# A four-layer graph network on one core: source logits taken from the projection, sums placed one chunk later, and a normalisation moved to ScalarE

## The chip, the core and the metric

The kernel runs on one core of a Trainium2 chip. The metric is the device time of one execution in microseconds (us); less is better. The engines of the core have short names in the profile: PE is TensorE (matmul), PEld its weight loads, DVE is VectorE, ACT is ScalarE, POOL is GpSimd, SP is SyncE, which here only issues transfers. A "q" behind a name (SPq, ACTq) means the sequencer that feeds the engine.

## What is computed

A graph with N = 2708 nodes and 256 features goes through four layers; each adds its result to the features and normalises the rows. Only layers 1 and 3 are touched by the change (layer 0 matters because layer 1's projection is computed inside its loop). Cut to that:

```python
x = layernorm(x + adj @ (x * W0))                        # layer 0
# layer 1: attention with 4 heads of 64 columns
h   = (x @ W).reshape(n, heads, head_dim)
src = einsum('nhd,d->nh', h, a[:head_dim, 0])            # source logits
dst = einsum('nhd,d->nh', h, a[head_dim:, 0])            # target logits
e   = src[:, :, None] + dst.T[None, :, :]
e   = where(e > 0, e, 0.2 * e)                           # leaky relu
attn = softmax(where(adj[:, None, :] > 0, e, -9e15))
out  = einsum('nhm,mhd->nhd', attn, h)
x = layernorm(x + layernorm(out) * gamma + beta)
# ... layer 2: a signed graph attention with 3 heads and two GRU cells ...
# layer 3
h = adj @ (x @ neigh_W.T) / (adj.sum(1) + 1)
x = layernorm(x + concatenate([x, h]) @ lin_W.T)
```

The 2708 nodes are 22 tiles of 128 rows (P = 128; the last tile has 20). adj is 2708 x 2708 and is read several times from the chip's main memory.

## The kernel before

It is a kernel in which each stage has been tuned by hand; a scheduler behind the language may move an instruction within the order of its engine, so the order in a trace is not always that of the text.

**Layer 1's softmax without a maximum.** Since exp(leaky(s + d)) is the larger of exp(s + d) and exp(0.2 (s + d)), a weight can be written, up to a factor of the row, as max(exp(-0.8 s), exp(0.8 d)) times exp(0.2 d). The kernel calls exp(-0.8 s) `fall` (one number per row and head, needed as a *row* that is spread over all partitions, `fall_b`), exp(0.8 d) `rise` (one number per partition) and folds exp(0.2 d) into the projected features `hs`. `fall` is therefore stored to a small array `fall_d` (4 x 2708) in main memory and loaded again, spread over 128 partitions.

**The projection of a tile, inside layer 0's loop** (`w1_a` holds, side by side, 4 columns for the source logits, 256 for the features and 4 for the target logits; H = 4, F = 256, FC = 2 blocks of 128):

```python
def layer1_projection(pool, t):
    n = sz(t)
    xt = transposed(ps_t, pool, xs[t], n, "xt")          # 2 PE transposes (tr), 1 ACT copy (L165)
    pm = ps_m.tile([P, 2 * F], F32, tag="pm", name="pm")
    for f in range(FC):
        nc.tensor.matmul(
            pm[:n, : F + H], xt[:, f, :n], w1_a[:, f, H:], start=(f == 0), stop=(f == FC - 1)
        )
    nc.scalar.activation(rise[:n, t, :], pm[:n, F : F + H], AF.Exp, scale=1.0 - ALPHA)
    nc.scalar.activation(hs[t][:n, :, HD], pm[:n, F : F + H], AF.Exp, scale=ALPHA)
    nc.vector.tensor_tensor(hs[t][:n, :, :HD], ...)
    pf = ps_t.tile([P, 4, P], F32, tag="tr", name="pf")
    for f in range(FC):
        nc.tensor.matmul(
            pf[:, 0, :n], w1_a[:, f, :P], xt[:, f, :n], start=(f == 0), stop=(f == FC - 1)
        )
    fall = pool.tile([H, P], F32, tag="fall", name="fall")
    nc.scalar.activation(fall[:, :n], pf[:H, 0, :n], AF.Exp, scale=ALPHA - 1.0)
    nc.gpsimd.dma_start(fall_d[:, t * P : t * P + n], fall[:, :n])
    # ... at the end of a span of tiles: load_fall(...) spreads fall_d over the partitions ...
```

In layer 0's loop TensorE does for each tile the strip (22 matmuls of 128x256, line 199), then the previous tile's tr, pm and pf. `load_strip` brings a strip of adj (1408 KB) into one of two buffers.

**Layer 1's main loop.** For two spans of target rows at a time (up to 1024 columns; three such groups), for two pairs of heads (`q`), over 22 chunks `c`:

```python
for c in range(NT):
    for i in range(2):                                    # DVE, L668
        nc.vector.scalar_tensor_tensor(p[:, :w], falls[g // 2][:, 2 * q + i, :w],
            rise[:, c, 2 * q + i : 2 * q + i + 1], mask[:, c, at : at + w], ALU.max, ALU.mult)
    for part in (heads, totals)[:: 1 if c % 2 == 0 else -1]:
        part(c, ps, ...)                                  # PE, L650 (acc) and L659 (den)
    step(c)                                               # one piece of the row work, below
    if c % 5 == 4 and degrees:
        row_degree(degrees.pop(0))                        # two ACT passes over a row of adj
```

**The row work between the chunks.** While a group runs, the rows that the group before has finished are normalised, and a part of layer 2 is prepared from them: for each tile its features times two vectors give u (128 x 3), u is split into three bfloat16 parts, and the edge mask P (a row of 2708, copied from fp8 to bfloat16) is multiplied with them ("the sums over P u", line 490, six matmuls named `pu`). Two buffers hold mask rows in turn. `step(c)` advances a generator; each `yield` is one chunk:

```python
def layer1_logits(pool, t, m, fill, split, gap):
    xt = transposed(ps_t, pool, xs[t], n, "xt")
    nc.gpsimd.dma_start(xt_d[g][:, :, at : at + n], xt[:, :, :n])
    fill(m, t)                                            # ACT, L560: the mask row of the tile
    yield
    own = m[:n, t * P : t * P + n]
    nc.vector.tensor_tensor(own, own, offdiag_h[:n, :n], ALU.mult)        # L573
    # ... pm (L576) = xt times uw on PE, u (L580) copied by ACT
    for i in range(3):                                    # L584, L587: five small operations
        split.tensor_copy(part, left)
        if i < 2:
            split.tensor_tensor(r[:n], left, part, ALU.subtract)
    for _ in range(gap):
        yield
    edge_part(t, m)                                       # PE, L490

if q == 1 and c % 2 == 0 and c // 2 < len(halves):        # in step(c): one tile every two chunks
    t = ended[c // 2][0]
    rows = two_rows[t % 2]
    steps.append(itertools.chain(
        halves[c // 2], [None], layer1_logits(l1, t, rows, mask_row, nc.gpsimd, 2)))
```

**Layer 3's rows.** When a block of layer 3 is summed up, its columns are turned back into rows and normalised (`moments` gives mean and 1 / standard deviation; the power -0.5 is on GpSimd, L151):

```python
pt = bank()
for f in range(FC):
    nc.tensor.transpose(pt[:n, f * P : (f + 1) * P], src[:, f, :n], ident)
nc.vector.scalar_tensor_tensor(o[:n], pt[:n, :F], rdeg[:n, t : t + 1], o[:n], ALU.mult, ALU.add)
layernorm(o, o, n)    # moments, then L157 on DVE: (o - mean) * rs
(nc.gpsimd if t % 2 else nc.sync).dma_start(out[t * P : t * P + n, :], o[:n])
```

Of the kernel before, what the change touches and what calls it, by code (L numbers as in the profile page):

```python
# [9 lines left out]
F32 = mybir.dt.float32  # L10
# [4 lines left out]
AF = mybir.ActivationFunctionType  # L15
ALU = mybir.AluOpType
# [3 lines left out]
P = 128  # L20
NEG_INF = -9000000000000000.0
HIGHEST = 3.0e38
ALPHA = 0.2
# [4 lines left out]
def kernel(  # L28
# [114 lines left out]
    def moments(src, n):  # L143

        bst = small.tile([P, 6], F32, tag="bn_st", name="bn_st")
        nc.vector.bn_stats(bst[:n], src[:n])
        mv = small.tile([P, 2], F32, tag="bn_mv", name="bn_mv", bufs=12)
        nc.vector.bn_aggr(mv[:n], bst[:n])
        rstd = small.tile([P, 1], F32, tag="bn_rs", name="bn_rs", bufs=12)
        nc.vector.tensor_scalar(rstd[:n], mv[:n, 1:2], EPS, None, ALU.add)  # L150
        nc.gpsimd.tensor_tensor(rstd[:n], rstd[:n], neg_half[:n], ALU.pow)  # L151
        return mv[:n, 0:1], rstd[:n]

    def layernorm(dst, src, n):

        mean, rs = moments(src, n)
        nc.vector.tensor_scalar(dst[:n], src[:n], mean, rs, ALU.subtract, ALU.mult)  # L157
# [154 lines left out]
    if True:  # L312
# [14 lines left out]
        if True:  # L327
# [5 lines left out]
# [3 lines that stand above are left out]
                pm = ps_m.tile([P, 2 * F], F32, tag="pm", name="pm")  # L336
                for f in range(FC):
                    nc.tensor.matmul(  # L338
                        pm[:n, : F + H], xt[:, f, :n], w1_a[:, f, H:], start=(f == 0), stop=(f == FC - 1)
                    )  # L340
                nc.scalar.activation(rise[:n, t, :], pm[:n, F : F + H], AF.Exp, scale=1.0 - ALPHA)
                nc.scalar.activation(hs[t][:n, :, HD], pm[:n, F : F + H], AF.Exp, scale=ALPHA)
                nc.vector.tensor_tensor(
                    hs[t][:n, :, :HD],
                    pm[:n, :F].rearrange("p (h d) -> p h d", d=HD),
                    hs[t][:n, :, HD:].to_broadcast([n, H, HD]),
                    ALU.mult,
                )
                pf = ps_t.tile([P, 4, P], F32, tag="tr", name="pf")
                for f in range(FC):  # L350
                    nc.tensor.matmul(
                        pf[:, 0, :n], w1_a[:, f, :P], xt[:, f, :n], start=(f == 0), stop=(f == FC - 1)
                    )
                fall = pool.tile([H, P], F32, tag="fall", name="fall")
                nc.scalar.activation(fall[:, :n], pf[:H, 0, :n], AF.Exp, scale=ALPHA - 1.0)
                nc.gpsimd.dma_start(fall_d[:, t * P : t * P + n], fall[:, :n])

                for g in [g for g, (lo, hi) in enumerate(spans[:4]) if hi == t + 1]:
                    load_fall(falls[g // 2], g, nc.gpsimd)
# [113 lines left out]
            if True:  # L473
# [138 lines left out]
                for g in range(0, len(spans), 2):  # L612
# [10 lines left out]
                    def step(c):  # L623
                        for s in list(steps):
                            if next(s, s) is s:
                                steps.remove(s)

                        if q == 0 and len(halves) < len(ended) and c > len(halves) * 8 // 3:
                            halves.append(layer1_end(l1, *ended[len(halves)]))
                            steps.append(itertools.islice(halves[-1], 2))  # L630
                            next(steps[-1])

                        if q == 1 and c % 2 == 0 and c // 2 < len(halves):
                            t = ended[c // 2][0]
                            rows = two_rows[t % 2]
                            steps.append(
                                itertools.chain(
                                    halves[c // 2], [None], layer1_logits(l1, t, rows, mask_row, nc.gpsimd, 2)
                                )
                            )  # L640
                            next(steps[-1], None)
# [253 lines left out]
    with (  # L895
# [332 lines left out]
        def rows3(u, y, o8):  # L1228

            a, w = units[u]  # L1230
            for h in range(2):
                for t, src in by_tiles(h * NH + a, w, lambda at, n: y[:, :, h, at : at + n], shared3):
                    n = sz(t)
                    o = o8[:, complete(u).index(t)]
# [3 lines that stand above are left out]
                    nc.vector.scalar_tensor_tensor(  # L1238
                        o[:n], pt[:n, :F], rdeg[:n, t : t + 1], o[:n], ALU.mult, ALU.add
                    )  # L1240
                    layernorm(o, o, n)
                    (nc.gpsimd if t % 2 else nc.sync).dma_start(out[t * P : t * P + n, :], o[:n])
                    yield

# [288 lines left out]
```

## Time and profile before

| What | Value |
|---|---|
| Time, median of 3 runs | 1970.05 us (1968.67 to 1974.76) |
| Span of the profiled execution | 1967.7 us |
| Layer 0 with layer 1's projections | until about 258 us |
| Layer 1's main loop | about 258 to 643 us |
| Layer 3's last matmul on TensorE | about 1941 us |
| Strip of adj, 1408 KB, issue to landing | 6.4 us median |
| Store of `fall`, 2 KB, issued by GpSimd | 22 times |
| Mask row's copy, L560, waiting for the sums | 28.9 us in 9 waits, longest 8.2 us |

How to read the profile's answers: the page's first part gives the busy time of each engine and its share of the span. The chain of work that ended last is followed back from the last instruction, at each step to what released it; in order of time its columns are start, length, engine, tile and line, and "x" with the number of instructions. The timeline gives for one engine start, length, line, operation, the tiles written and read, and in brackets how long the engine idled before and what ended that idle time. The windows give the busy time of each engine in a stretch of the span.

### The profile page before, as it was taken

How to read it: one execution, taken by the hardware profiler on the slowest of the kernel's cores; microseconds unless marked ns; L12 is line 12 of the kernel's file. 1: busy time of each engine (PE TensorE's matmuls, PEld its weight loads, DVE VectorE, ACT ScalarE, POOL GpSimd, SP SyncE). 2: the span in 40 equal slices, each digit the busy share in tenths (PEclk: the TensorE clock that was granted, in tenths of full speed). 3: DMA queues.
4: the chain of work that ended last, by engine and by line, in shares of the span. 5: the costliest groups of instructions: out<-in, count | busy, mean ns of one | idle time of the engine just before them, and what ended most of it. 6: DMA issues, size and time to landing. Idle time of an engine off the chain costs nothing.

```text
span 1967.7 us, 21033 instructions
## 1 busy us (share of the span) xinstructions
PE 1895.1 (96%) x7028; PEld 945.7 (48%) x7028; DVE 1454.0 (74%) x2364; ACT 852.0 (43%) x1011; POOL 348.8 (18%) x522
## 2 busy tenths in 40 slices
PE   8999999999999999999999999999999999999995
PEld 7888822222333444445545444444445555554443
DVE  5333378898897689999987888585877758745764
ACT  0100045445603367777855656555655555211000
POOL 0211210013515302111210101020110201311211
PEclk9999999999999999999999999999999999999998
DMA  8343333432200786766475756454554535633752
GB/s 288 121 169 140 139 114 126 152 119 97 69 4 19 211 266 221 245 219 202 126 214 164 215 161 180 114 162 120 149 153 119 130 100 136 168 108 105 199 153 78
DMA packets 398210, 293.96 MB, mean 149 GB/s; under 512 B 105354, under 2 KB 379434, under 8 KB 390244
## 3 DMA queue, kind: packets, MB, share of 16 engines
q1 hardware_dynamic: 381180, 237.86, 41.2%
q0 software_dynamic: 10848, 50.23, 7.5%
q10 hardware_dynamic: 6064, 4.42, 0.7%
q8 instruction: 58, 0.95, 0.2%
q14 instruction: 60, 0.49, 0.1%
HBM read 280.03 MB, written 12.40 MB: 149 GB/s over the span
## 4 chain that ended last, share of the span: by engine, by line
PE 70%; DVE 17%; issue 5%; DMA 3%; POOL 2%; ACT 1%; SPq 1%; ACTq 0%; DVEq 0%; POOLq 0%
PE m L996 31%; PE acc L650 9%; PE acc L199 9%; DVE z L852 8%; PE bank L1056 6%; PE den L659 5%; PE bank L1032 3%; PE bank L1107 2%; DVE p L668 2%; DVE none L848 1%; POOL bn_rs L151 1%; PE acc L423 1%; PE pm L338 1%; DMA p<-in_adj_t_dram 1%; SPq L934 1%
## 5 line engine op out<-in xcount | busy, mean ns | idle before, releaser
L668 DVE SCALAR_TENSOR_TENSOR p<-fall_b,rise,mask 128x1024 f32<-128x1024 f32 (+1 forms) x264 | 298.5, 1152 | 37.1 <-PE den L659 18.6
L1198 ACT ACTIVATE p<-st,e_neg 128x1024 f32<-128x1024 f32 (+1 forms) x198 | 197.5, 1040 | 186.1 <-PE m L996 183.6
L996 PE MATMUL m<-p,xq 128*128 128x512 f32 (+1 forms) x528 | 245.6, 547 | 0.8 <-DVE p L984 0.6
L650 PE MATMUL acc<-p,h 128*64 128x512 f32 (+2 forms) x1056 | 228.4, 561 | 3.2 <-DVE p L668 2.7
L996 PE MATMUL m<-s,xq 128*128 128x512 f32 (+1 forms) x528 | 224.7, 542 | 0.4 <-DVE s L985 0.4
L852 DVE CUSTOM_DVE_ANT_0 z<-e_b,none 128x2708 f32<-128x2708 f32 (+1 forms) x66 | 196.7, 2983 | 0.3 <-DVE e_b L822 0.2
L857 ACT ACTIVATE z<-z,st 128x2708 f32<-128x2708 f32 (+1 forms) x66 | 168.5, 2553 | 64.7 <-DVE st L852 63.1
L199 PE MATMUL acc<-turn,strip 128*128 128x256 f32 (+1 forms) x836 | 187.1, 379 | 0.0
L1201 ACT ACTIVATE p<-p 128x1024 f32<-128x1024 f32 (+1 forms) x198 | 179.5, 943 | 0.3
L996 PE MATMUL m<-p,x 128*128 128x512 f32 (+1 forms) x396 | 169.5, 547 | 2.6 <-DVE p L1202 2.6
L1202 DVE TENSOR_TENSOR p<-p,blk 128x1024 f32<-128x1024 f32 (+1 forms) x132 | 142.6, 1095 | 30.9 <-ACT p L1201 16.3
L199 PEld LDWEIGHTS acc<-turn,strip 128*128 128x128 f32 (+1 forms) x836 | 151.9, 185 | 23.5 <-issue 0.2
L262 PE MATMUL s<-blk,x 128*128 128x512 f32 (+2 forms) x416 | 162.9, 545 | 0.0
L983 DVE TENSOR_TENSOR s<-p 128x512 f32<-128x512 f32 (+1 forms) x132 | 82.8, 628 | 97.9 <-PE m L996 83.8
L996 PEld LDWEIGHTS m<-p,xq 128*128 128x128 f32 x528 | 99.3, 191 | 99.6 <-issue 74.6
L996 PEld LDWEIGHTS m<-s,xq 128*128 128x128 f32 x528 | 98.7, 190 | 93.6 <-issue 70.3
L650 PEld LDWEIGHTS acc<-p,h 128*64 128x64 f32 x1056 | 65.2, 137 | 149.5 <-issue 119.8
L659 PE MATMUL den<-p,h 128*32 128x512 f32 (+2 forms) x1056 | 125.9, 557 | 2.3 <-DVE p L668 2.2
L151 POOL TENSOR_TENSOR bn_rs<-bn_rs,neg_half 128x1 f32<-128x1 f32 (+1 forms) x110 | 79.3, 722 | 242.3 <-DVE bn_rs L150 239.4
L262 PEld LDWEIGHTS s<-blk,x 128*128 128x128 f32 x416 | 77.9, 190 | 74.2 <-issue 62.5
L996 PEld LDWEIGHTS m<-p,x 128*128 128x128 f32 x396 | 74.6, 191 | 76.7 <-issue 59.1
L165 ACT COPY xt<-tr 128x256 f32<-128x256 f32 (+1 forms) x44 | 16.0, 363 | 209.2 <-PE tr L163 203.5
(228 smaller groups left out, 2587.5 us busy)
## 6 DMA issues: line engine op xcount, KB each, us to landing
blk<-in_adj_t_dram SPq DMA_DIRECT2D x172, 256.0 KB, 3.8
turn<-in_adj_dram SPq DMA_DIRECT2D x22, 1354.0 KB, 6.0
strip<-in_adj_t_dram SPq DMA_DIRECT2D x19, 1408.0 KB, 6.4
blk<-in_adj_t_dram SPq DMA_DIRECT2D x88, 192.0 KB, 3.9
turn<-in_adj_t_dram SPq DMA_DIRECT2D x65, 256.0 KB, 4.0
arow<-in_adj_dram POOLq DMA_DIRECT2D x10, 1354.0 KB, 6.7
turn<-in_adj_dram POOLq DMA_DIRECT2D x10, 1354.0 KB, 7.2
blk<-in_adj_t_dram SPq DMA_DIRECT2D x103, 128.0 KB, 2.6
```

The lines of the kernel that those rows point to most:

```text
L199: nc.tensor.matmul(acc, s[:, c, :n], rhs(c), start=(c == 0), stop=(c == NT - 1))
L262: nc.tensor.matmul(acc[f][:, :w], xs[c][:, f * P : (f + 1) * P], s[:, c - c0, :w], start=(c == 0), stop=(c == NT - 1),)
L650: nc.tensor.matmul(acc[s][i * HD : (i + 1) * HD, :ws], hs[c][:, 2 * q + i, :HD], ps[i][:, p0 : p0 + ws], **flags,)
L659: nc.tensor.matmul(den[j : j + CT, :ws], hs[c][:, 2 * q + i, HD + 1 - CT :], ps[i][:, p0 : p0 + ws], **flags,)
L668: nc.vector.scalar_tensor_tensor(p[:, :w], falls[g // 2][:, 2 * q + i, :w], rise[:, c, 2 * q + i : 2 * q + i + 1], mask[:, c, at : at + w] ...
L852: nc.vector.tensor_tensor_reduce(out=z[:n], in0=e_b[:n, k, :], in1=none[:n], scale=-1.0, scalar=HIGHEST, op0=ALU.add, op1=ALU.min, accum_o ...
L857: nc.scalar.activation(z[:n], z[:n], AF.Exp, scale=-1.0, bias=st[:n, t, 0, k : k + 1], accum_out=den[:n])
L996: nc.tensor.matmul(dst[:, :w], lt, rt, start=start, stop=stop)
L1056: nc.tensor.matmul(g[:, :w], lt, rt, start=(q == 0), stop=(q == len(terms) - 1))
L1198: nc.scalar.activation(p[:, :, :w], st_k[:, :, :w], AF.Relu, scale=-1.0, bias=e_neg[:, at, k : k + 1])
L1201: nc.scalar.activation(p[:, :, :w], p[:, :, :w], AF.Exp, scale=-1.0)
L1202: made = nc.vector.tensor_tensor(p[:, :, :w], p[:, :, :w], blk[:, i, :, :w], ALU.mult)
```

## The change

It has three parts.

1. *Source logits.* The projection `pm` takes all 264 columns of `w1_a`, so the source logits come out as 4 more columns, with nodes on partitions. The two matmuls `pf`, which gave the same numbers with nodes along the columns, are gone. `fall` is now 128 x 4, and one transfer, issued by ScalarE, turns it while storing it: 512 single numbers into the four rows of `fall_d`. This is meant to take work from TensorE in layer 0.
2. *Sums over P u.* The gap between the making of u and the sums grows from two chunks to three, so that the split parts of u are there when TensorE comes to them.
3. *Layer 3's rows.* The last step of the normalisation, (o - mean) * rs, goes from VectorE to ScalarE as rs * o + (-mean * rs); VectorE makes the small factor -mean * rs.

```diff
-                        pm[:n, : F + H], xt[:, f, :n], w1_a[:, f, H:], start=(f == 0), stop=(f == FC - 1)
+                        pm[:n, : F + 2 * H], xt[:, f, :n], w1_a[:, f], start=(f == 0), stop=(f == FC - 1)
                     )
-                nc.scalar.activation(rise[:n, t, :], pm[:n, F : F + H], AF.Exp, scale=1.0 - ALPHA)
-                nc.scalar.activation(hs[t][:n, :, HD], pm[:n, F : F + H], AF.Exp, scale=ALPHA)
+                nc.scalar.activation(rise[:n, t, :], pm[:n, F + H : F + 2 * H], AF.Exp, scale=1.0 - ALPHA)
+                nc.scalar.activation(hs[t][:n, :, HD], pm[:n, F + H : F + 2 * H], AF.Exp, scale=ALPHA)
+                fall = pool.tile([P, H], F32, tag="fall", name="fall", bufs=4)
+                nc.scalar.activation(fall[:n], pm[:n, :H], AF.Exp, scale=ALPHA - 1.0)
                 nc.vector.tensor_tensor(
                     hs[t][:n, :, :HD],
-                    pm[:n, :F].rearrange("p (h d) -> p h d", d=HD),
+                    pm[:n, H : H + F].rearrange("p (h d) -> p h d", d=HD),
 ...
-                pf = ps_t.tile([P, 4, P], F32, tag="tr", name="pf")
-                for f in range(FC):
-                    nc.tensor.matmul(
-                        pf[:, 0, :n], w1_a[:, f, :P], xt[:, f, :n], start=(f == 0), stop=(f == FC - 1)
-                    )
-                fall = pool.tile([H, P], F32, tag="fall", name="fall")
-                nc.scalar.activation(fall[:, :n], pf[:H, 0, :n], AF.Exp, scale=ALPHA - 1.0)
-                nc.gpsimd.dma_start(fall_d[:, t * P : t * P + n], fall[:, :n])
+
+                with nc.allow_non_contiguous_dma("a row of each head"):
+                    nc.scalar.dma_start(fall_d[:, t * P : t * P + n].rearrange("h n -> n h"), fall[:n])
 ...
-                                    halves[c // 2], [None], layer1_logits(l1, t, rows, mask_row, nc.gpsimd, 2)
+                                    halves[c // 2], [None], layer1_logits(l1, t, rows, mask_row, nc.gpsimd, 3)
 ...
-                    layernorm(o, o, n)
+                    mean, rs = moments(o, n)
+                    nc.vector.scalar_tensor_tensor(mean, mean, -1.0, rs, ALU.mult, ALU.mult)
+                    nc.scalar.activation(o[:n], o[:n], AF.Identity, scale=rs, bias=mean)
```

## What I expect, before seeing the result

> **What bounds the kernel now.** I read the page's first part, then the chain of work that ended last, then the three stretches that the change touches: windows, timeline and waits of each.
>
> The page says that TensorE is the bound almost everywhere:
>
> ```profile
> span 1967.7 us, 21033 instructions
> PE 1895.1 (96%) x7028; PEld 945.7 (48%) x7028; DVE 1454.0 (74%) x2364; ACT 852.0 (43%) x1011; POOL 348.8 (18%) x522
> ```
>
> TensorE lacks only 73 us of the span. So two things can bring time: instructions taken from TensorE where it is busy, and waits of TensorE that end sooner. Work taken from another engine brings nothing unless that engine ends the chain.
>
> *Layer 0, 66 to 252 us.* The chain, in order of time, in one tile of the steady stretch (start, length, what; a float32 matmul leaves two records, so x4 is two matmuls and a strip's 22 matmuls are 44 records):
>
> ```profile
> 130.68 0.22 PE tr L163 x2
> 130.89 0.87 PE acc L199 x4
> 131.76 0.88 PE pm L338 x4
> 132.64 0.44 PE pf L351 x4
> 133.08 8.64 PE acc L199 x40
> ```
>
> The sum is 11.05 us, and the windows give TensorE busy for 11.04 of the 11.04 us from 121.04 to 132.08. No gap: whatever leaves TensorE here leaves the span. The two pf matmuls, which make the source logits with 124 of 128 output rows unused, are 0.44 us.
>
> *Layer 1, 258 to 640 us.* The timeline of TensorE shows it idle in few places. The largest and two of the regular ones (in brackets the idle time before the instruction, and what ended it):
>
> ```profile
> 471.50 0.62 PE L490 MATMUL pu<-turn,u_parts 128*32 128x512 bf16 x3 [2.62 <-POOL u_parts L584]
> ...
> 607.71 0.56 PE L490 MATMUL pu<-turn,u_parts 128*32 128x512 bf16 x6 [1.07 <-POOL u_parts L584]
> 614.31 0.56 PE L490 MATMUL pu<-turn,u_parts 128*32 128x512 bf16 x6 [1.07 <-POOL u_parts L584]
> ```
>
> They are the sums over P u, which stand in TensorE's queue before GpSimd has split u into three bfloat16 parts. All of this kind: 2.62 at 471, then 0.28, 0.43, 1.07, 1.07, 0.36 and 1.07 between 592 and 627, together 6.9 us. The cause of the second group is a ring, seen in the timelines of ScalarE and GpSimd:
>
> ```profile
> 608.31 2.45 ACT L560 CAST turn<-mask 128x2708 bf16<-128x2708 fp8e4 x1 [3.25 <-PE pu L490]
> 610.66 0.15 ACT L580 COPY u<-pm 128x3 f32<-128x3 f32 x1
> ...
> 613.35 0.90 POOL L584 CAST u_parts<-u_left 128x3 bf16<-128x3 f32 x1
> ```
>
> The sums of one tile (607.71) free one of the two mask rows; the copy of a later tile's mask (608.31) waits for that; the next tile's u (610.66) stands behind this copy on ScalarE; GpSimd's five steps follow (610.88 to 614.25); and the next sums start at 614.31. One turn is 6.6 us, and TensorE has about 5.65 us of work in it.
>
> *The end, from 1941 us.* TensorE is done; the last tiles' rows go one after another through VectorE and GpSimd:
>
> ```profile
> 1949.94 0.41 DVE L157 TENSOR_SCALAR o<-o,bn_mv,bn_rs 128x256 f32<-128x256 f32 x1 [0.72 <-POOL bn_rs L151]
> 1951.53 0.41 DVE L157 TENSOR_SCALAR o<-o,bn_mv,bn_rs 128x256 f32<-128x256 f32 x1 [0.34 <-POOL bn_rs L151]
> 1953.13 0.41 DVE L157 TENSOR_SCALAR o<-o,bn_mv,bn_rs 128x256 f32<-128x256 f32 x1 [0.35 <-POOL bn_rs L151]
> ```
>
> One tile each 1.6 us, and each time VectorE waits for GpSimd's power.
>
> **What the Trainium skill says.** (1) "SBUF — State Buffer", section "Who interferes with whom": VectorE with two SBUF inputs and GpSimd reading SBUF share ports under an exclusive lock. The trace agrees: GpSimd's splits of 128x3 take 0.19 us or about 1.2 us, the latter beside L668 (1.28 us, two SBUF tensors). So the length of the split chain is a matter of luck, 1 to 4.5 us, and slack is the right cure. (2) "DMA: Bandwidth & Descriptors", section "Rules for kernel authors": a transfer whose last dimension is not contiguous becomes one descriptor per element. No transfer before the change is of this kind; the new store is, 128 x 4 = 512 descriptors of 4 bytes. (3) Same page, "Issuing engines are not separate DMA queues": ScalarE's and SyncE's transfers run on the same 16 engines. So 32 descriptors per engine and tile lie beside the strip's 1.4 MB. (4) "ScalarE: Activation LUTs", section "What ACT_TABLE_LOAD costs": 186 ns + 0.833 ns per column, about 93 ns more for each per-partition operand. The trace's 128x256 copy (L165) is 363 ns against the page's 399, so I estimate 0.55 us for the new normalisation with its two operands, against VectorE's 0.41 us.
>
> **Part 1, the source logits.** Removed: pf, 0.44 us a tile. Added: pm with 264 columns for 260, 0.88 x 4/260 = 0.013 us. Net 0.43 us of TensorE a tile, new period 10.61 us. Tile 21's pf is not on the path (after it VectorE's first p, 2.47 us, ends the wait), so 21 tiles: 21 x 0.43 = 9.0 us. ScalarE's small exponential goes from 0.27 (4x128) to about 0.17 us (128x4, like L341). GpSimd loses 22 issues of 0.55 us, hidden before too. ScalarE gets the issue instead: SyncE's issues of transfers in many pieces take 0.37 to 0.55 us, and ScalarE must first see its own exponential finished. In the steady stretch ScalarE idles 8.6 of 11 us. Only tiles 0 to 2, at 50 to 57 us, stand back to back (2.4 us each): there the next tile's copy to xt stands behind the issue, and TensorE has 0.86 us of strip to bridge a delay that I put at 1.2 us: minus 0.35 us, three times. Net gain 8.0 us, up to 9.0 if the order spares it.
>
> Does the store hurt the strips? A strip lands 5.8 to 6.3 us after its issue and is needed 10.2 us after it. By the page's queue table the first queue's 381180 packets took 41.2% of 16 engines' span, 0.412 x 16 x 1967.7 / 381180 = 34 ns each; 32 small ones per engine would then be 1.1 us. It fits.
>
> **Part 2, sums three chunks behind u.** A chunk is 2.8 us in the last group (5.65 over two) and about 3.5 us around 470 to 530. One chunk more exceeds every single wait (at most 2.62), and u now stands ahead of the mask copy that waits for the sums: the ring opens. Upper bound 6.9 us. But VectorE is not far behind: for two chunks in the last group four p of 0.87, and 0.41 + 0.48 + 0.42 + 0.18 + 0.20 + 0.15 of rows, 5.3 us, and 0.6 us of waiting for GpSimd's power: 5.9 against TensorE's 5.65. And the mask row is held a chunk longer: the copy (2.45 us) must fit between the sums of a tile and the multiplication with the off-diagonal on VectorE, one chunk later, where two chunks were free before. VectorE would stand there for some tenths. I keep 2.5 of the 4.3 us in the last group, 2.5 of the 2.62 at 471, and take off 1 us for new waits between 480 and 530, where ScalarE also has row sums of twice 2.46 us: net 4 us.
>
> **Part 3, layer 3's rows.** In its main part TensorE is the bound and nothing changes. At the end VectorE's loop loses 0.41 and gains a 128x1 operation of about 0.15 us: 0.26 x 5 tiles = 1.3 us less. Against that every store waits for ScalarE, about 0.35 us later (0.15 + 0.06 + 0.55 - 0.41); GpSimd issues three of them between its powers, and the last store ends the span: 4 x 0.35 = 1.4 us. Net zero.
>
> Sum: 8.0 + 4 + 0 = 12 us, 1970 - 12 = 1958 us.
>
> **Rivals.** *A: the small descriptors hold up the strips.* If a piece of 4 bytes took six times the mean packet, 200 ns, 32 of them would be 6.4 us, the strip would land at 12 us and each of 18 tiles would lose about 2 us: 36 us, time near 1998. For it: 512 pieces for 2 KB. Against: the transfers took only 0.36 of the engines' time in that window. *B: the mask rows become the wait.* If ScalarE's row sums stand ahead of the mask copy, VectorE stands still at its multiplication, p come late, and the 6.9 us come back as waits for L668: 1962. For it: the copy waited for the sums already, up to 8.2 us, 28.9 in all. Against: no wait of VectorE for it in the loop so far. *C: everything hidden by TensorE is truly free*: 9.0 + 6.9 + 1 = 17 us, 1953.
>
> **Range and chances.** C and B bound the likely part, 1953 to 1962; below it I leave 3 us for loads that happen to fall better later, above it 5 us for half a case A or a worse order in the loops. Faster by over 2% would need 39 us, more than twice the upper bound: 0.02. Slower by over 2% needs A in full: 0.03.
>
> **What will show it.** Right: the chain of a tile without pf and a period of 10.6 us; layer 1 starting about 8 us sooner; no wait of L490 for u_parts between 450 and 640, and the loop's end another 4 us sooner; the end after TensorE's last matmul as long as now. Wrong: TensorE waiting for the strip (A); VectorE waiting for L560, and L650 or L659 for p (B); ScalarE's copy to xt late by more than 1 us in each tile.

## The result: 3.5% slower, and the profile after

| | before | after |
|---|---|---|
| Time, median of 4 runs each on the same chip | 1972.4 us (1968.67 to 1979.16) | 2042.4 us (2038.0 to 2047.39) |
| Ratio, with 95% interval | | 1.035 (1.031 to 1.040) |
| Span of the profiled execution | 1967.7 us | 2036.1 us |
| Layer 1's first p on VectorE | 258.4 us | 321.8 us |
| Layer 1's last p | 640.0 us | 710.7 us |
| Layer 3's last sum on VectorE (s) | 1938.0 us | 2008.1 us |
| From there to the end | 29.7 us | 28.0 us |

The landmarks say where the 68 us of the two spans are: +63.4 until layer 1 starts, +7.3 in layer 1's loop (381.6 to 388.9), nothing between there and layer 3's end (70.7 and 70.1 us late), and -1.7 at the end. Part 1 of the change works before the first landmark, so layer 0 is read first.

Two lines of the page of the kernel before: a group of instructions with its busy time, the mean of one in ns and the idle time before it; and an issue of transfers with its size and its median time to landing in us.

```profile
L199 PE MATMUL acc<-turn,strip 128*128 128x256 f32 (+1 forms) x836 | 187.1, 379 | 0.0
...
strip<-in_adj_t_dram SPq DMA_DIRECT2D x19, 1408.0 KB, 6.4
```

The page of the kernel after: span, the engines' busy time, and the same two lines, the first now with what ended the idle time.

```profile
span 2036.1 us, 20830 instructions
PE 1900.6 (93%) x6940; PEld 948.4 (47%) x6940; DVE 1443.2 (71%) x2364; ACT 860.7 (42%) x1033; POOL 325.8 (16%) x500
...
L199 PE MATMUL acc<-turn,strip 128*128 128x256 f32 (+1 forms) x836 | 199.1, 396 | 50.8 <-DMA strip<-in_adj_t_dram 50.8
...
strip<-in_adj_t_dram SPq DMA_DIRECT2D x19, 1408.0 KB, 15.9
```

TensorE now waits 50.8 us for the strips of adj, before the matmuls of line 199; before the change it did not wait for them at all. The strip needs 15.9 us to land where it needed 6.4.

The chain of waits of the kernel after, in order of time (start, length, what). It answers to the tile of 11.05 us in the prediction:

```profile
123.64 19.60 DMA strip<-in_adj_t_dram
143.24 0.04 issue
143.28 2.08 PE acc L199 x4
145.36 1.76 PE pm L338 x4
147.12 9.68 PE acc L199 x40
156.80 0.22 PE tr L163 x2
157.02 0.86 PE acc L199 x4
157.89 0.89 PE pm L338 x4
```

Three things are in it. There is no pf, as meant. The chain passes through the transfer: 19.6 us from issue to the first matmul that needed it. And after the wait TensorE is slow for a while: pm takes 1.76 us right after it and 0.89 us a tile later. The 0.86 us of the last acc x4 in the chain can't be set beside the 2.08, since the chain shows only the part of it that does not overlap its neighbours. By the timeline, with full lengths, the same four records take 2.08 us after this wait and 1.03 us where nothing was waited for, and pm 1.97 and 1.05: about twice as long. In this profile all nine waits for a strip (2.49 to 8.85 us) are followed by such slow matmuls. The view by windows shows a lower clock (columns: stretch, length, busy time of PE, PEld, DVE, ACT, POOL with instructions, granted clock, DMA share, GB/s). The first fence is the kernel before, the second the kernel after; both stretches begin at 66 us, and their ends, 252 and 315 us, stand at the same point of the work.

```profile
66.00:252.00 186.00, 186.00 (x909) 159.83 (x908) 70.52 (x135) 19.40 (x69) 35.20 (x56) 1.00 0.41 147
```

```profile
66.00:315.00 249.00, 198.19 (x836) 164.16 (x835) 65.14 (x132) 15.65 (x66) 24.02 (x38) 0.90 0.75 110
```

The stretch grew by 63 us: 50.8 us is TensorE standing still, 12.2 us is TensorE busy for longer, although pf is gone. Without pf, at full clock, the work would be about 186 - 17 x 0.43 = 178.7 us; at a clock of 0.90 that is 178.7 / 0.90 = 198.6 us, and 198.2 us was measured. So the waits cost about 51 us, the lower clock after them about 20 us, and the removed pf gave about 7 us back. The DMA engines' share of busy time went from 0.41 to 0.75 while they moved fewer bytes in each microsecond (110 for 147 GB/s).

The timeline of the kernel after shows the transfers of that tile (start, length, engine, line, tiles; in brackets the idle time and what ended it):

```profile
125.96 0.37 ACTq L353 DMA_DIRECT2D fall_d<-fall  x1
...
143.28 2.08 PE L199 MATMUL acc<-turn,strip 128*128 128x256 f32 x4 [8.85 <-DMA strip<-in_adj_t_dram]
144.69 0.79 POOL L331 DMA_DIRECT2D fall_b<-fall_d  x1 [18.27 <-DMA fall_d<-fall]
```

The small store was issued 2.3 us after the strip (125.96 after 123.64) and landed 1.4 us after it (144.69, when GpSimd, which waited for it, could go on). A store of 2 KB was under way for 18.7 us, and a strip of 1408 KB beside it.

### The profile page after: what moved, and what is told of

It reads as the page before. It is cut to its first block, busy times and chain, and to the rows that moved or that the text cites. A ratio compares the mean times of both kernels' runs of the same rounds, so it can differ in the third digit from the quotient of the medians.

```text
span 2036.1 us, 20830 instructions
## 1 busy us (share of the span) xinstructions
PE 1900.6 (93%) x6940; PEld 948.4 (47%) x6940; DVE 1443.2 (71%) x2364; ACT 860.7 (42%) x1033; POOL 325.8 (16%) x500
## 4 chain that ended last, share of the span: by engine, by line
PE 61%; DVE 16%; DMA 12%; issue 4%; ACT 3%; POOL 2%; SPq 1%; ACTq 0%; DVEq 0%; POOLq 0%
PE m L993 29%; DVE z L849 7%; PE acc L647 7%; DMA strip<-in_adj_t_dram 7%; PE bank L1053 6%; PE acc L199 6%; PE den L656 4%; PE bank L1029 3%; DMA turn<-in_adj_dram 2%; PE bank L1104 2%; DVE none L845 1%; DVE p L665 1%; PE acc L420 1%; ACT turn L594 1%; POOL bn_rs L151 1%
## 5 line engine op out<-in xcount | busy, mean ns | idle before, releaser
L199 PE MATMUL acc<-turn,strip 128*128 128x256 f32 (+1 forms) x836 | 199.1, 396 | 50.8 <-DMA strip<-in_adj_t_dram 50.8
L199 PEld LDWEIGHTS acc<-turn,strip 128*128 128x128 f32 (+1 forms) x836 | 161.0, 195 | 80.9 <-DMA strip<-in_adj_t_dram 52.9
L854 ACT ACTIVATE z<-z,st 128x2708 f32<-128x2708 f32 (+1 forms) x66 | 168.5, 2553 | 64.3 <-DVE st L849 62.5
L364 DVE TENSOR_SCALAR mask<-strip 128x2816 fp8e4<-128x2816 f32 (+3 forms) x37 | 36.5, 997 | 146.9 <-DMA strip<-in_adj_t_dram 146.8
## 6 DMA issues: line engine op xcount, KB each, us to landing
strip<-in_adj_t_dram SPq DMA_DIRECT2D x19, 1408.0 KB, 15.9
```

Source lines behind the costliest of these rows:

```text
L199: nc.tensor.matmul(acc, s[:, c, :n], rhs(c), start=(c == 0), stop=(c == NT - 1))
L854: nc.scalar.activation(z[:n], z[:n], AF.Exp, scale=-1.0, bias=st[:n, t, 0, k : k + 1], accum_out=den[:n])
```

## Experiments

### Which part of the change loses the time

Three kernels (e1, e2, e3) each have one part of the change alone. Part 1:

```diff
 kernel before, with part 1 of the change and nothing else
+ pm[:n, : F + 2 * H] ...;  fall[:n] = exp(...) of pm[:n, :H]
+ nc.scalar.dma_start(fall_d[:, t * P : t * P + n].rearrange("h n -> n h"), fall[:n])
- pf, two matmuls;  nc.gpsimd.dma_start(fall_d[:, ...], fall[:, :n])
```

> The kernel before with part 1 alone (source logits as columns of the projection, stored turned by ScalarE). Theory S (the store of 512 pieces of 4 bytes is at fault): nearly the whole loss is here, about 2040 us, strips landing after about 16 us instead of 6, and the first p of layer 1 near 320 us instead of 258. Theory G (the longer gap or the order that follows from it is at fault in layer 1): this one loses 63 us in layer 0 but layer 1's loop from first to last p stays at 381 to 382 us, since the gap is as before; theory S in its strict form says that the loop too grows to about 389 us, because the last stores delay the first rows of adj that ScalarE sums up and ScalarE's copies out of the accumulators stand behind those sums.

Measured: 2056.4 us, ratio 1.041 (1.038 to 1.044). Strips land after 17.8 us in the median, TensorE waits 61.5 us for them in ten waits, layer 1 starts at 335.6 us and its loop takes 390.2 us. So part 1 alone has the whole loss, the longer loop of layer 1 included. It costs even 14 us more than the three parts together (84 for 70 us), with runs from 2043.2 to 2058.0 us here and from 2038.0 to 2047.4 us there. No run shows why.

Part 2:

```diff
- halves[c // 2], [None], layer1_logits(l1, t, rows, mask_row, nc.gpsimd, 2)
+ halves[c // 2], [None], layer1_logits(l1, t, rows, mask_row, nc.gpsimd, 3)
```

> The kernel before with part 2 alone (sums over P u three chunks behind u). My prediction's step: 4 us faster, 1966 to 1967, no wait of L490 for the split of u in layer 1's loop except at most a part of the first. Theory G: 5 to 7 us slower, 1976 to 1979, with VectorE waiting for the mask row's copy or TensorE for x. What the profile of the changed kernel suggests: the first wait of 2.6 us stays, the regular waits of 1.07 us turn into smaller ones of 0.5 us for the split and 0.66 us for the rows on VectorE: gain 0 to 2 us.

Measured: 1970.4 us, ratio 0.9998 (0.9987 to 1.0009): nothing. The loop of layer 1 takes 380.8 us for 381.6. The timeline of TensorE in this kernel shows why:

```profile
472.63 0.40 PE L490 MATMUL pu<-turn,u_parts 128*32 128x512 bf16 x3 [2.62 <-POOL u_parts L584]
...
534.12 1.98 PE L650 MATMUL acc<-p,h 128*64 128x384 f32 x12 [1.86 <-ACT sum L682]
...
608.19 0.56 PE L490 MATMUL pu<-turn,u_parts 128*32 128x512 bf16 x6 [0.53 <-POOL u_parts L584]
616.68 0.44 PE L163 MATMUL tr<-ident,x 128*128 128x128 f32 x2 [0.65 <-DVE x L557]
623.01 0.44 PE L163 MATMUL tr<-ident,x 128*128 128x128 f32 x2 [0.66 <-DVE x L557]
```

The longest wait, 2.62 us, is still there to the hundredth. Of the waits between 592 and 627 us two of about half a microsecond are left (0.48 and 0.53), and after these the sums don't wait; then TensorE waits 0.65 us in each turn for VectorE's rows (x, line 557). Two turns are 6.33 us apart where they were 6.6 (the transposes at 616.68 and 623.01). In layer 1's whole loop the waits for the split of u fell from 6.9 to 4.0 us. Against that stand 2.0 us of waiting for x, 2.7 in two waits for ScalarE's copies of sums (one of 1.86 us is shown) and 0.5 for xt, none of which were there before. The waits were mostly turned into others.

Part 3:

```diff
- layernorm(o, o, n)
+ mean, rs = moments(o, n)
+ nc.vector.scalar_tensor_tensor(mean, mean, -1.0, rs, ALU.mult, ALU.mult)
+ nc.scalar.activation(o[:n], o[:n], AF.Identity, scale=rs, bias=mean)
```

> The kernel before with part 3 alone (layer 3's rows finished by ScalarE). My prediction's step: 0 us. What the profile of the changed kernel suggests: from the last s of the last block to the end 29.5 us instead of 31.2, so 1.5 to 2 us faster, with the loop of a tile at the end 0.95 to 1.7 us instead of 1.2 to 1.9.

Measured: 1970.9 us, ratio 0.9998 (0.9986 to 1.001). From the start of the last sum's last step to the end this profile has 27.8 us for 29.7 (the expectation counts from its first step: 29.5 for 31.2). Its timeline at the end:

```profile
1951.90 0.16 DVE L1242 SCALAR_TENSOR_TENSOR bn_mv<-bn_mv,bn_rs 128x1 f32<-128x1 f32 x1 [0.33 <-POOL bn_rs L151]
...
1952.84 0.16 DVE L1242 SCALAR_TENSOR_TENSOR bn_mv<-bn_mv,bn_rs 128x1 f32<-128x1 f32 x1 [0.47 <-POOL bn_rs L151]
```

VectorE waits for GpSimd's power in every tile, as before the change; ScalarE's operation takes 0.60 us. A gain of up to 2 us in one profile is less than these runs can tell from nothing.

### Is it the missing pf or the store?

The next kernel (e4) keeps the source logits as columns of pm, but TensorE turns them: the tiles of a span are collected as 128 x 16, one transpose for the span (six in all) makes rows of them, and GpSimd stores rows of 512 bytes as the kernel before did.

```diff
+ nc.scalar.activation(fall_c[:n, t], pm[:n, :H], AF.Exp, scale=ALPHA - 1.0)
+ # once for each span lo..hi of tiles
+ nc.tensor.transpose(pf[:m, 0, :], fall_c[:, lo:hi].rearrange("p t h -> p (t h)"), ident)
+ nc.scalar.copy(fall[:m], pf[:m, 0, :])
+ for t in range(lo, hi): nc.gpsimd.dma_start(fall_d[:, t * P : ...], fall[at : at + H, :n])
- nc.scalar.dma_start(fall_d[:, t * P : t * P + n].rearrange("h n -> n h"), fall[:n])
```

> Part 1 without its store: the projection takes all 264 columns, the exponential is 128x4 as in the changed kernel, but once per span of tiles (six times) TensorE turns the 128x16 numbers by one transpose and ScalarE copies them, and GpSimd stores rows of 512 bytes as before. Theory S: the strips land after 6 us as before, the period of a tile is 10.6 us, and TensorE's saving of 0.43 us a tile stays: 21 x 0.43 less six transposes of about 0.15 is 8 us, time near 1963. If taking pf away brings nothing (a wait of another kind takes its place), the time stays at 1971.

Measured: 1962.8 us, ratio 0.9960 (0.9947 to 0.9973). This is faster than the kernel before. Its chain of waits in layer 0 is again TensorE without a gap:

```profile
98.00 8.63 PE acc L199 x40
108.61 8.63 PE acc L199 x40
119.13 9.06 PE acc L199 x42
130.17 8.63 PE acc L199 x40
...
161.91 9.06 PE acc L199 x42
```

From 98.00 to 108.61 is 10.61 us, the period that the prediction worked out for a tile without pf. Four tiles with their one transpose take 42.78 us (119.13 to 161.91), which is 4 x 10.61 and 0.34 us for the transpose and what goes with it. Layer 1 starts 6.3 us sooner than before (252.1 us).

So the matmuls were worth what they seemed; what loses is the store.

### The store alone, beside a kernel that doesn't need it

The nine kernels that follow are the kernel before, whole, with one more store in each tile of layer 0, of data that nobody reads: `rise`, 128 x 4 numbers, issued by ScalarE. Only the place of the pieces in main memory differs.

```diff
+ beside_d = dram.tile([H, N], F32, name="beside_d")
  nc.gpsimd.dma_start(fall_d[:, t * P : t * P + n], fall[:, :n])
+ nc.scalar.dma_start(beside_d[:, t * P : t * P + n].rearrange("h n -> n h"), rise[:n, t, :])
```

> The kernel before, whole, with one extra store per tile in layer 0: ScalarE stores rise, 128 x 4, turned into an array of 4 x 2708 that nobody reads: 512 pieces of 4 bytes. Every theory of the store itself (not of its missing pf, nor of a wait for its data) must have the loss back: the strips of adj land at 15 to 17 us from issue instead of 6.3, layer 1 starts at 318 to 340 us instead of 258, time near 2050. If instead strips stay near 6.3 us and time near 1970, the loss comes from what waits for the stored data (the loads of fall), not from the writes.

Three others change the array and the view:

```diff
 d2: [N, H],       beside_d[t * P : t * P + n, :]           <- rise[:n, t, :]
 d3: [N, H, 128],  beside_d[t * P : t * P + n, :, 0]        <- rise[:n, t, :]
 d4: [H, N],       beside_d[:2, ...] turned                 <- rise[:n, t, :2]
```

> The same extra store with the same 2 KB, but not turned: 128 pieces of 16 bytes. Theory W (each small write costs a fixed time at the memory, some 20 ns one after another, whatever its size): a quarter of the delay, 2 to 3 us a tile; strips land at 8 to 9 us, still below the 10.2 us at which they are needed, time 1970 to 1985. Theory Q (any second transfer in small pieces beside a strip takes the engines from it): nearly the full delay, strips at 13 us or more, time above 2020. Theory L (only pieces whose neighbours share a block of memory with other engines' pieces are slow): 16-byte neighbours also share blocks, so delayed as in W.

> The same 512 pieces of 4 bytes, but each goes to its own block of 512 bytes in main memory. Theory W: as slow as the turned store, strips at 15 us or more, time near 2050. Theory L (several engines write into one block of memory and wait for each other): the delay goes, strips near 6.5 to 8 us, time 1970 to 1980.

> The turned store for two of the four heads: 256 pieces of 4 bytes. Theory W: half the delay, some 5 us more per strip, landing at 11 to 12 us, which is 1 to 2 us later than needed; 15 to 40 us over the kernel before, time 1985 to 2010. A cost per transfer instead of per piece: as the full turned store, near 2050.

d3 took 1971.1 us and d1 2052.3, at the same number and size of pieces. So what counts is where they land. d2 and d3 go against theory W, which had 8 to 9 us and 15 us or more for their strips where 6.1 and 6.2 were measured, and d2 against theory Q too; d2's neighbours share blocks of memory, so it goes against theory L's first form as well. Five more follow; four hold the turned order and only widen the step:

```diff
 s1: [H, N, 128]  beside_d[:, t * P : t * P + n, 0] turned   (512 bytes apart)
 s2: [H, N, 16]   the same                                   (64 bytes apart)
 x2: [H, N, 4]    the same                                   (16 bytes apart)
 x1: [H, N, 2]    the same                                   (8 bytes apart)
 s3: [N, H, 2]    beside_d[t * P : t * P + n, :, 0]          (8 bytes apart, a node's four together)
```

> The kernel before with the extra store in the turned order (for each head a row over the nodes), but each of the 512 pieces of 4 bytes in its own 512 bytes. Theory L (pieces that share a block of memory wait for each other): as the spread store d3, strips near 6.3 us, time 1966 to 1975. If the order is what hurts, with the four pieces of a node far apart, and d3 was fast only for its order: strips above 12 us, time above 1990.

> The same turned order, pieces 64 bytes apart, so eight of them share 512 bytes and none shares 64. Theory L with a block of 64 bytes or less: fast, 1966 to 1975. With a block of 512 bytes: a delay between none and the full one, strips at 8 to 16 us, time 1975 to 2050, as eight pieces instead of 128 meet in each block.

> 512 pieces of 4 bytes in the order of the nodes: the four of one node stand 8 bytes apart within 32 bytes, node beside node, 4 KB a tile; 8 pieces share 64 bytes and 64 share 512. If any two pieces in one block of memory hurt each other: slow, strips above 10 us, time above 1985. If only many engines that write into one block at the same moment hurt each other: fast, 1966 to 1976, since what stands close comes from one partition or its neighbours.

> The same with pieces 16 bytes apart: 4 of them share 64 bytes, from 4 neighbouring partitions. By the Trainium skill (DMA: Bandwidth & Descriptors, The descriptor swizzle) four neighbouring partitions belong to one transfer engine. If meetings of different engines count: fast, store near 4.5 us, strips near 6.3 us, time 1967 to 1973. If any pieces of different partitions in 64 bytes hurt: between s2 and x1, strips at 7 to 10 us.

> The extra store in the turned order with pieces 8 bytes apart, so that 8 of them share 64 bytes, as in s3, but here they come from 8 partitions and one head, in s3 from 2 partitions and four heads. If the number of pieces in 64 bytes is what counts: as s3, strips near 7.2 us, store near 6.2 us, time near 1972. If pieces from different partitions, moved by different transfer engines at the same moment, are what counts: between s3 and d1, store landing at 8 us or more, strips at 10 us or more, time above 1980.

All measurements together; landings are medians in us from issue, of the strips between 60 and 300 us and of the extra store; one run each, against 1969 to 1972 us for the kernel before on the same chips.

| Extra store, pieces | Bytes from piece to piece | In 64 bytes | Store lands | Strip lands | Time |
|---|---|---|---|---|---|
| none (kernel before) | | | | 6.3 | 1970 |
| 512 of 4 bytes, turned (d1) | 4 | 16 | 16.6 | 17.0 | 2052.3 |
| 256 of 4 bytes, turned (d4) | 4 | 16 | 9.0 | 12.5 | 1992.6 |
| 512, turned (x1) | 8 | 8 | 8.7 | 8.2 | 1971.8 |
| 512, nodes in order (s3) | 8 | 8 | 6.2 | 7.2 | 1972.0 |
| 512, turned (x2) | 16 | 4 | 5.0 | 6.4 | 1976.3 |
| 512, turned (s2) | 64 | 1 | 4.4 | 6.2 | 1970.6 |
| 512, turned (s1) | 512 | none | 4.2 | 6.1 | 1971.2 |
| 512, nodes in order (d3) | 512 | none | 4.3 | 6.2 | 1971.1 |
| 128 of 16 bytes, in order (d2) | 16 | 4 | 4.1 | 6.1 | 1967.4 |

x1 and s3 fell between the readings that their expectations had set apart: x1's store at 8.7 us as for meetings of transfer engines, but its strips at 8.2 us and not 10 or more, and its time not above 1980; s3's strips at 7.2 us, neither fast nor above 10.

The tile view of the strip in two of them: first the turned store, dense (d1), then the same 512 pieces 64 bytes apart (s2); the waits are of that tile, in us and times.

```profile
  PE acc L200: 44.2, 9
...
DMA to landing us min/median/max: 5.9/17.0/22.1
```

```profile
  DVE mask L370: 45.2, 16
...
DMA to landing us min/median/max: 5.8/6.2/7.4
```

In the first TensorE waits for the strip nine times, 44.2 us; in the second no line has TensorE waiting for it, only VectorE's mask, as in the kernel before, which costs nothing.

What follows:

- The store is enough for the whole loss. Added to the kernel before, where nothing waits for its data, it costs 83 us (2052.3 for 1969.1, one run).
- It is not the number of pieces, nor their size, nor the turned order, nor that ScalarE's transfers run beside SyncE's. All of these are the same in d1 and s1, and s1 costs nothing.
- It is where the pieces lie, and the dense ones are slow. In the turned order, over a landing of 4.2 us, the store takes 0.2, 0.8, 4.5 and 12.4 us more with 1, 4, 8 and 16 pieces in 64 bytes: more than in proportion. At the dense end that is 12.4 us / 512 = 24 ns for each piece, as if they went one after another. Half the pieces (d4) take 4.8 us more, 19 ns each. In this series the distance, the number of pieces in 64 bytes and the whole stretch written (2 KB in d1, 256 KB in s1) change together, and no step between 16 and 64 bytes was run. So a block of just 64 bytes is not shown.
- Who writes beside whom seems to have a smaller part. x1 and s3 both have eight pieces in 64 bytes; with pieces from eight nodes the store lands at 8.7 us, with two nodes' at 6.2. It is one pair of single runs, and it differs in the order as well; with 512 bytes between pieces the order made no difference (d3 4.3, s1 4.2 us). The Trainium skill, "DMA: Bandwidth & Descriptors", section "The descriptor swizzle", has four neighbouring partitions on one transfer engine for a transfer to 128 partitions; if that holds for this store, in x1 two engines write into the same 64 bytes, in d1 four, in x2, s3 and d2 one. The order of the table fits that, but the trace doesn't say which engine moved which piece, and x2 and s3 are not free of delay, so it is not shown that meetings of engines are the mechanism. What the memory does with such writes stays open.
- Delay is not yet loss. With x1 the strips land 2 us later than before, at 8.2 us, and the time is that of the kernel before; with d4 they land at 12.5, past the 10.2 us at which TensorE needs them, and 23 us are lost. How far the strip is delayed does not follow from the store's own landing alone: x1's and d4's stores land alike (8.7 and 9.0 us), their strips do not (8.2 and 12.5). Why is open. x2's 1976.3 us is one run, within what single runs of the kernel before gave (1965.6 to 1979.2), and its layer 1 starts at 258.9 us (before: 258.4); I take no cause from it.

### Versions that could keep the gain

The layout that was free (d2: 16 bytes of each node) can carry the real data: `fall_d` becomes 2708 x 4, the spread copy in SBUF has the four heads of a node side by side, and VectorE reads every fourth number.

```diff
- fall_d = dram.tile([H, N], F32, name="fall_d")
+ fall_d = dram.tile([N, H], F32, name="fall_d")
- nc.scalar.dma_start(fall_d[:, t * P : t * P + n].rearrange("h n -> n h"), fall[:n])
+ nc.scalar.dma_start(fall_d[t * P : t * P + n, :], fall[:n])
- falls[g // 2][:, 2 * q + i, :w]
+ falls[g // 2][:, :w, 2 * q + i]
```

> The change's first part with the store's layout changed: fall_d is 2708 x 4, so the store writes 128 pieces of 16 bytes as in d2, the loads spread contiguous rows over the partitions, and VectorE reads every fourth number of fall_b in layer 1. If the layout of the store is the whole cause: strips at 6.1 to 6.6 us, layer 1 starts 7 to 9 us sooner than before (249 to 251 us), 1960 to 1963 in all, slightly below the turn by TensorE (1962.8). If VectorE's reading with a stride costs: L668 goes from 1.28 to 1.5 us or more for 1024 columns, VectorE becomes the bound of layer 1, and its loop grows from 381.6 us by 10 us or more: time above 1970.

Measured: ratio 1.080 (1.076 to 1.084), some 158 us slower than the kernel before. The store behaves (strips 5.9 us, layer 1 starts at 251.8 us, 6.6 us sooner), but the tile view of p shows a price (count, shortest/median/longest in ns, first and last start, then the shapes; first the kernel before, then this one):

```profile
L668 DVE SCALAR_TENSOR_TENSOR p<-fall_b,rise,mask x264: 867/1276/1495, 258.4 to 640.0; 128x1024 f32<-128x1024 f32 x88, 128x660 f32<-128x660 f32 x44
```

```profile
L668 DVE SCALAR_TENSOR_TENSOR p<-fall_b,rise,mask x264: 1331/2101/2412, 251.8 to 842.3; 128x1024 f32<-128x1024 f32 x88, 128x660 f32<-128x660 f32 x44
```

The median mixes two shapes. By shape, the mean of a 128x1024 operation went from 1280 to 2207 ns and that of a 128x660 one from 896 to 1401 ns: a step of 16 bytes in one of two inputs makes VectorE's largest operation of layer 1 72% and 56% longer, and the loop takes 590.5 us instead of 381.6. The Trainium skill, "SBUF — State Buffer", section "Door 1: The DMA port swizzle", speaks of 16-byte lines in SBUF with a penalty for each access that goes to a new line. A step of four float32 goes to a new line at every number, and the longer times agree with that. The same section, though, names four float32 as how far one can step for free; here a step of exactly four was not free, and the measurement decides.

A slower VectorE is only part of the loss. The page has TensorE waiting for ScalarE, and the chain has one operation of GpSimd in it:

```profile
L650 PE MATMUL acc<-p,h 128*64 128x512 f32 (+2 forms) x1056 | 239.0, 574 | 124.8 <-ACT sum L682 62.5
```

```profile
277.16 159.43 POOL rdeg L598
```

That is a step of the row degree, one number in each of 128 partitions, which took 0.2 to 1.3 us in the kernel before. Here it lasts 159 us, from 277.16 to 436.62 us. From 260.44 to 436.56 us VectorE runs its p one after another without a pause, where it paused for 0.23 to 0.33 us after every two p in the kernel before; GpSimd ends just when VectorE stops. ScalarE's row sums stood 91.8 us behind GpSimd, its copies of sums behind them, and TensorE stood still 62.5 us in one piece. It fits the lock between VectorE and GpSimd of the prediction's point (1). No run tests it, and spans on GpSimd are rough. The profiled execution is a slow one of 2177.5 us; the ratio is from the two quickest of six, 2121.8 and 2136.0 us.

The last version (x3) is the turn by TensorE with the change's parts 2 and 3, both edits as shown above:

> The turn by TensorE (e4) together with parts 2 and 3 of the change. If the parts add up as measured alone (e4 -7.2 us; parts 2 and 3 -0.4 us each, which their intervals don't tell from zero): 1961 to 1964. If the earlier start of layer 1 or the other order lets part 2 work after all: 1956 to 1960. If part 2 only moves waits about: not different from e4's 1962.8.

Measured: 1962.0 us (1961.15 to 1964.85), ratio 0.9953 (0.9940 to 0.9967). It can't be told apart from the turn alone (0.9960, the intervals overlap): what parts 2 and 3 add lies within the measurement. Both beat the kernel before by 0.4 to 0.5%, and the changed kernel by about 80 us.

## Why the prediction was wrong, step by step

**"Does the store hurt the strips? ... 34 ns each ... It fits": this step failed, and with it the result.** I worked out the cost of a piece as the mean time of all packets of a queue, 34 ns, and so 1.1 us for 32 pieces on each engine. The strip landed 10.8 us later instead (17.1 for 6.3 us), 10.8 / 32 = 338 ns for a piece on each engine, ten times as much. That mean was of SyncE's transfers, whose packets are mostly of 512 bytes; no store of single numbers was among them, so it held no information on this one. The sentence "No transfer before the change is of this kind" is not quite so: four loads of biases at the start (`braw`, line 221) move 768 single numbers each, and two of them landed after 5.6 and 6.2 us. But these read small pieces from main memory and write none there, so they would not have priced the store.

The records of the small pieces don't show the cost either: in d1 and s1 alike they are listed with 9 ns. The packets of the strip beside them do. Their median is 422 ns before and after, but in the stretches of the two windows above their mean went from 486 to 1236 ns, and the slowest tenth from 640 ns or more to 3284 ns or more (d1 has 1254 and 3531, s2 490 and 670). And in the kernel after the pieces of the store issued at 125.96 us start between 132.82 and 135.28 us, while the store landed at 144.69, 9.4 us after the last of them.

**Rival A is what happened, and larger than A.** I gave it 200 ns a piece, a landing of 12 us and 36 us of loss; it was 338 ns, 17.1 us and 63 us until layer 1. Of its picture one thing was missing: after each of the nine waits of this profile TensorE runs slower for some microseconds (2.08 us for what takes 1.03), and the lower clock costs about 20 us in sum. The argument against it, "the transfers took only 0.36 of the engines' time", was of one tile (0.41 over the whole stretch), and it was no argument: the share rises with the delay (0.75 after). With 512 pieces for 2 KB known beforehand and no trace of such a store, a chance of 0.03 was too low.

**Part 1's gain on TensorE was right.** The period of 10.61 us came as worked out (the fence of the turn by TensorE). In the version with 16-byte rows, which has no transposes and no delay, TensorE needs 196.9 us from the first strip's first matmul to the long run of the last strip (39.34 to 236.29), where the kernel before needs 205.3 us (38.41 to 243.72): 8.4 us over 20 tiles, 0.42 us each for the 0.43 predicted. Layer 1 starts only 6.6 us sooner in that profile, because layer 0 began 0.9 us later there and about 0.8 us was lost in the last two tiles. So the term of 8.0 was right to about half a microsecond.

**Part 2's net gain of 4 us was mis-sized: it is none.** The upper bound of 6.9 us was rightly named, and the reason to doubt it too ("VectorE is not far behind: ... 5.9 against TensorE's 5.65"), but I drew the wrong sum from it. A chain of VectorE and GpSimd at 5.9 us, and ScalarE's row copies, were standing just behind the split of u; a turn shrank only from 6.6 to 6.33 us, and then it waited for VectorE's rows. That the longest wait, 2.62 us, stays was not foreseen. The traces show part of it: the first three of these sums start 6.45 us after their tile's pm in both kernels (465.04 and 471.50 before, 466.18 and 472.63 with part 2), so the longer gap did not move them there. u, copied at 467.30 us behind ScalarE's row sum, goes through GpSimd's five steps until 472.58, three of them about 1.2 us each beside L668. Why the order stayed is open.

**Part 3's zero was right in the time.** VectorE's small operation took 0.16 us for the estimated 0.15, ScalarE's 0.60 us for 0.55; the end is 1.7 to 1.9 us shorter in the profiles and the time is the same in the runs.

**Rivals B and C** did not come: no wait of VectorE for the mask row carries the loss, and hidden work was not all free.

**Layer 1's loop, 7.3 us longer**, was in no step. It belongs to the store (8.6 us longer with part 1 alone, 6.4 with the extra store of d1, none with the turn by TensorE). In the page of the kernel after the first group's matmuls wait for ScalarE's copies of sums:

```profile
L647 PE MATMUL acc<-p,h 128*64 128x512 f32 (+2 forms) x1056 | 228.5, 564 | 12.1 <-ACT den L683 6.6
```

ScalarE is then still at row sums of adj, whose loads were late like the strips: the first of these loads was issued at 316.94 us and took 15.95 us, so that the first row sum starts 11.2 us after layer 1's first p, at 332.98 us; in the kernel before it starts 1.7 us after it. The longest wait of the group, 6.63 us, is at 394.58 us, where the first pair of heads gives way to the second. I read this from the traces; no run took it apart.

## What to carry to other kernels

A small store can be the most expensive transfer of a stage. Before using a transfer to turn data, look at where neighbouring pieces land: 512 numbers of 4 bytes set side by side in memory by a transposing view made the strips beside them land 10 us later; the same numbers in 16-byte pieces, or 64 bytes apart, cost nothing here. And look at who reads the array afterwards: the layout with 16-byte pieces cost more in layer 1 (some 158 us in all) than the dense store had in layer 0. Turn small data where it is cheap and dense, here with one TensorE transpose for four tiles (0.27 us by itself, 0.34 us in the period), and store rows. And price a new kind of transfer by a trace of that kind, not by the mean of a queue that holds none of it; where there is no such trace, put the doubt into the chances.

## What the runs showed of the hardware that I had not expected

- The cost of 4-byte writes to main memory depends on where they lie: 512 of them land in 4.4 us when 64 bytes apart and in 16.6 us when side by side, beside the same traffic.
- That cost falls on other transfers beside it: a strip of 1408 KB landed after 17.0 us instead of 6.3 because of 2 KB.
- In the trace the small piece's own time doesn't show it: 9 ns for the fast and for the slow ones. The strip's packets do (mean 486 ns before and 1236 ns after the change).
- After 8.85 us of waiting TensorE needed 2.08 us for what takes 1.03, and the mean granted clock of the whole stretch fell from 1.00 to 0.90: a wait can cost more than its length. Not every wait did: in d4 five of six (0.64 to 3.82 us) left 1.13 us for the same records, and one of 2.91 us left 1.91.
- An operation of VectorE on 128 x 1024 took 2.21 us instead of 1.28 (means) when one of its two large inputs was read at every fourth float32.
- While VectorE ran such operations without a pause, an operation of GpSimd on one number per partition lasted 159 us, where the same took 0.2 to 1.3 us before.
